# Block products for the first group's values and keys, and its queries by batch, in the opening of an attention and mixture-of-experts kernel

## The chip, the cores and the metric

The kernel runs on one core of a Trainium2 chip. The core has five engines with a queue of instructions each: TensorE (PE, matrix products), VectorE (DVE), ScalarE (ACT), GpSimd (POOL) and SyncE (SP, which issues DMA transfers). Within a queue the order is the program's. The metric is the device time of one execution in microseconds (us); the median of three runs before the change is 695.65 us.

## What is computed

Sixteen batches of 128 tokens with 256 features go through a cross attention with 16 heads of 64, and then through a top-1 mixture of eight experts with a shared expert. Keys and values come from two normalised sources, the context and the tokens ("latents"), 128 rows each; queries come from the tokens alone.

```python
def attention(x, latents, shift, scale, ln1_w, ln1_b, ln2_w, ln2_b, Wq, Wkv, Wo):
    x = layer_norm(x, ln1_w, ln1_b)                       # the context, 16 x 128 x 256
    lat = layer_norm(latents, ln2_w, ln2_b)
    lat = lat * (1.0 + scale[:, None, :]) + shift[:, None, :]
    q = einsum('bld,ed->ble', lat, Wq)
    kv = einsum('bld,ed->ble', concatenate((x, lat), axis=-2), Wkv)
    k, v = split(kv, 2, axis=-1)
    q, k, v = to_heads(q), to_heads(k), to_heads(v)       # 16 heads of 64
    logits = einsum('bhqd,bhkd->bhqk', q * attn_scale, k * attn_scale)
    out = einsum('bhqk,bhkd->bhqd', softmax(logits), v)
    return einsum('ble,de->bld', out.transpose(0, 2, 1, 3).reshape(b, n2, INNER), Wo)

x = x + attention(ctx_1024, layernorm(x), cond_1024, cond_1024, ...)
x = x + mixture_of_experts(layernorm(x), ...)
```

All data are float32.

## The kernel before

The attention goes by groups of two batches (g = 0 to 7), and each group by four steps: step u is batch u % 2 of the group and half (u // 2) % 2 of the heads. A step issues the logits of its eight heads (`logits`, L907, tile S), takes row maxima on DVE (`maxima`, L919), exponentials with sums on ACT (`exponents`, L926), divides on POOL (`normalise`, L939), transposes blocks on DVE (`turn`, L948) and sends them through memory and back with DMAs on SP's queue (`turn`, `fetch`), and ends with the product of the step before it with its values (`weigh`, L972, tile O). Between these, PE makes what later steps need: queries, keys and values.

Inputs of a group are normalised, transposed on PE and scaled into `kvT`, [128 features, chunk c, batch i, context or tokens, 128 rows]. For the first group `first_inputs(i)` does this for one batch at a time (transposes L695, tile fkvt); for the second group `inputs(1)` gives eight pieces on DVE and `transpose(c)` (tile kvt, L623); later groups are transposed through memory.

There are two ways to make keys and values. `k_plain(b, h, m)` and `v_plain(b, h, t)` multiply directly, one batch at a time: per half of the heads and group 16 instructions of 256 columns for the keys, 8 of 512 columns for the values. `Seven` makes one half for both batches of a group from seven products of blocks instead of eight (n = 1 to 7, two instructions of 256 columns each, banks X, Y and Z). It needs sums and differences of blocks of the weights (`weight_sums`, `weight_difference`, on POOL) and of the tokens (`token_sums`, POOL), and puts the products together with copies on ACT (`hold`) and sums on DVE (`join`, `join_held`). Before the change the first group uses `Seven` for its second values only (step 2); its first values and all its keys are plain.

PSUM banks come from pools: `ps_m` (tag mm) has three, `ps_s` (tag S) two, `ps_o` (tag O) one. A bank is written again only after the readers of what it held.

The order on every engine is written out by hand, `tc.manual_schedule`, so the program's order is the queue's. The opening runs: `first_inputs(0)`; four pieces of keys of batch 0 (L1322 to L1324); `first_inputs(1)`; one piece of values; the eight pieces of `inputs(1)` on DVE; the queries of both batches, four units (`q_unit`, L734); then step 0 and step 1 by `plain_step`, with the rest of the keys and values in them; step 2 and on by `seven_step`. In `first_inputs(0)` the inverse root starts from ACT's square root (L671); in `first_inputs(1)` it is found on DVE alone (`newton`). The weights are loaded on SP's queue: two quarters of the keys' weights (wk), the second batch's tokens, the other two quarters, the values' weights (wv, 1 MB), the queries' (wq, 1 MB, in the tile named early).

Of the kernel before, what the change touches and what calls it, by code (L numbers as in the profile page):

```python
# [9 lines left out]
F32 = mybir.dt.float32  # L10
# [7 lines left out]
P = 128  # L18
# [9 lines left out]
def resampler_attn__then__top1_moe_kernel(  # L28
# [476 lines left out]
    with ExitStack() as at:  # L505
# [41 lines left out]
        load_keys(0)  # L547
        load_keys(1)
        nc.sync.dma_start(out=xres[0][:, 1, :], in_=x[1])
        load_keys(2)  # L550
        load_keys(3)
        nc.sync.dma_start(
            out=wv, in_=wkv_t[:, INNER : 2 * INNER].rearrange("(c p) e -> p c e", p=P)
        )
        nc.sync.dma_start(out=wq, in_=wq_t.rearrange("(c p) e -> p c e", p=P))

        def later_loads():
            nc.sync.dma_start(out=wr[:, :, 0:E], in_=router.rearrange("(c p) e -> p c e", p=P))
# [20 lines left out]
        def inputs(g):  # L579
# [73 lines left out]
        def first_inputs(i):  # L653
# [11 lines left out]
            nc.vector.tensor_scalar(  # L665
                v[:, 1:2], mv[:, 1, 1:2], 1.0 + EPS, EPS * EPS, ALU.mult, ALU.add
            )
            if i == 0:

                root = small.tile([P, 2], F32, name="froot")  # L670
                nc.scalar.activation(root, v, AF.Sqrt)  # L671
                half = small.tile([P, 2], F32, name="fhalf")
                nc.vector.tensor_scalar(half, v, -0.5, None, ALU.mult)
                y = small.tile([P, 2], F32, name="fy")
                nc.vector.reciprocal(y, root)
                a = small.tile([P, 2], F32, name="fa")
                nc.vector.tensor_tensor(a, y, y, ALU.mult)
                nc.vector.tensor_tensor(a, a, half, ALU.mult)
                r = small.tile([P, 2], F32, name="fr")
                nc.vector.scalar_tensor_tensor(r, a, 1.5, y, ALU.add, ALU.mult)  # L680
# [66 lines left out]

        def q_unit(g, j):
            for jj in range(2):
                q_piece(g, j, jj, ps_m, "mm")  # L750
            q_keep(g, j)

        def keys_in_blocks(o, i):

# [441 lines left out]

            nc.scalar.activation(spare[0:1, 1:2], spare[0:1, 0:1], AF.Exp)

        def plain_step(u, units, side=(), behind=()):

            units, side = list(units), list(side)
# [7 lines left out]
            if u == 0 or u >= 2 * B - 2:  # L1209
                recall_exp()  # L1210
            if u > 1:
                keep_heads(u - 2)
            nm = maxima(u, 0, ps[0])
            exponents(u, 0, ps[0], nm)
            nm = maxima(u, 1, ps[1])
            if u > 1:
                exponents(u, 1, ps[1], nm)
                for n in range(2):
                    normalise(u, n)
                turn(u, 0)  # L1220
                unit(2)
                turn(u, 1)
                fetch(u)
                unit()
                weigh(u - 1)
                keep_heads(u - 1)
                unit(3)
                for f in behind:
                    f()
                finish(B - 2)  # L1230
                unit(len(units))
                return
# [12 lines left out]
            fetch(u)  # L1245
            for f in behind:
                f()
            unit()
            if u > 0:
                weigh(u - 1)  # L1250

# [79 lines left out]
        weight_sums(v_block, v_sums, 0, nc.gpsimd)  # L1331
        pieces, transpose = inputs(1)
        v_plain(0, 0, 0)
        for f in pieces:
            f()
        for j in range(4):
            q_unit(0, j)

        def second_inputs(c):
            transpose([c])  # L1340
# [4 lines left out]
        for g in range(NG):  # L1345
# [16 lines left out]
            scaled = t_on(("t_scale", 0), ("t_scale", 1))  # L1362

            if g == 0:
                turn_c = [lambda c=c: second_inputs(c) for c in range(DC)]
                ks = [lambda m=m: k_plain(1, 0, m) for m in range(2)]
                plain_step(
                    0,
                    [ks[0], turn_c[0], ks[1], turn_c[1]]
                    + [lambda: v_plain(0, 0, 1), lambda: v_plain(1, 0, 0), lambda: v_plain(1, 0, 1)],  # L1370
                )
                weight_sums(k_block, k_sums, 0, nc.gpsimd)
                token_sums(0, nc.gpsimd)
# [7 lines left out]
                seven_step(  # L1381
                    2, Seven("v", 0, 1), ask[2:], {1: kept[3]},
                    (
                        roots, (), (),
                        [lambda: token_sums(1, nc.gpsimd), lambda: weight_difference(k_block, 0, nc.gpsimd)]
                        + scaled,
                    ),
                )
                ask, kept = asking(1, 1)
                seven_step(  # L1390
                    3, Seven("k", 1, 0), ask, kept, turns,
                    on("t_fetch")
                    + [
                        lambda: weight_difference(v_block, 0, nc.gpsimd),
                        lambda: weight_sums(k_block, k_sums, 1, nc.gpsimd),
                        lambda: weight_difference(k_block, 1, nc.gpsimd),
                    ],
                )
                continue
            had_t, had_h = g + 1 < NG, g > 1  # L1400
# [22 lines left out]
            if g + 1 < NG:  # L1423
                ask, kept = asking(g + 1, 0)
                seven_step(
                    u + 2, Seven("v", g, 1), ask, kept,
                    (h_on("h_stats", "h_variances"), roots, (), ()), scaled,
                )
                ask, kept = asking(g + 1, 1)
                seven_step(  # L1430
                    u + 3, Seven("k", g + 1, 0), ask, kept, turns, t_on("t_fetch") + h_on("h_scale")
                )
            else:
                seven_step(
                    u + 2, Seven("v", g, 1), (), {}, (h_on("h_stats", "h_variances"), (), (), roots),
                    [shared_unit] * 2,
                )
                plain_step(
                    u + 3, [shared_unit] * 7, [],
                    [now["h_scale"], now["h_turn"], now["h_fetch"], spare_sums, route_consts, up_sums],  # L1440
                )
        weigh(2 * B - 1)
# [849 lines left out]
```

## Time and profile before

| | us |
|---|---|
| median of three runs (695.04 to 696.1) | 695.65 |
| the profiled execution, its own time | 695.21 |
| its span | 693.5 |
| logits of step 0, 1, 2, 3 start at | 24.5, 36.1, 45.3, 57.6 |
| wv landed | 12.0 |
| context of the second group issued on SP's queue | 12.9 |
| last product on PE ends | 687.3 |

The times in the table's last four rows are counted from the span's start. In a timeline row the first number is the start, the second the duration from the first to the last instruction of the group, then engine, line, operation, output and inputs, the shape, the number of records, and in brackets how long the engine was idle before it and what it waited for. A matmul instruction of float32 data leaves two records, a transpose one. In the first 45 us PE, DVE, ACT and POOL are busy for 43.3, 27.4, 21.9 and 19.9 us.

### The profile page before, as it was taken

How to read it: one execution, taken by the hardware profiler on the slowest of the kernel's cores; microseconds unless marked ns; L12 is line 12 of the kernel's file. 1: busy time of each engine (PE TensorE's matmuls, PEld its weight loads, DVE VectorE, ACT ScalarE, POOL GpSimd, SP SyncE). 2: the span in 40 equal slices, each digit the busy share in tenths (PEclk: the TensorE clock that was granted, in tenths of full speed). 3: DMA queues.
4: the chain of work that ended last, by engine and by line, in shares of the span. 5: the costliest groups of instructions: out<-in, count | busy, mean ns of one | idle time of the engine just before them, and what ended most of it. 6: DMA issues, size and time to landing. Idle time of an engine off the chain costs nothing.

```text
span 693.5 us, 12756 instructions
## 1 busy us (share of the span) xinstructions
PE 684.8 (99%) x4390; PEld 585.9 (84%) x4390; DVE 462.4 (67%) x1033; ACT 361.3 (52%) x1084; POOL 357.9 (52%) x549
## 2 busy tenths in 40 slices
PE   9999999999999999999999999999999999999996
PEld 6778888888888888888888887887888899988995
DVE  6667677777678688678758657647736467766520
ACT  3556466466555655655556556514436455545540
POOL 4249446546545446436435534512566477867751
PEclk9999999999999999999999999999999999999999
DMA  8255846765866685695694485543592257667513
GB/s 268 71 201 187 236 166 197 225 208 183 213 218 196 189 250 178 212 226 172 215 229 166 158 299 169 179 106 47 172 335 63 28 113 188 161 150 202 125 21 79
DMA packets 141834, 121.34 MB, mean 175 GB/s; under 512 B 61377, under 2 KB 127426, under 8 KB 141762
## 3 DMA queue, kind: packets, MB, share of 16 engines
q1 hardware_dynamic: 135602, 111.46, 52.7%
q0 software_dynamic: 5584, 8.20, 6.8%
q8 instruction: 37, 0.61, 0.4%
q10 hardware_dynamic: 576, 0.79, 0.4%
q14 instruction: 35, 0.29, 0.1%
HBM read 71.66 MB, written 48.92 MB: 174 GB/s over the span
## 4 chain that ended last, share of the span: by engine, by line
PE 91%; DVE 3%; ACT 2%; DMA 2%; issue 1%; POOL 0%; POOLq 0%; DVEq 0%; SPq 0%; ACTq 0%
PE O L972 8%; PE S L907 8%; PE pw L991 8%; PE pq L734 8%; PE rD L1858 6%; PE rX L2024 5%; PE skX L853 5%; PE svX L853 5%; PE rYZ L2024 4%; PE skZ L853 3%; PE skY L853 3%; PE svZ L853 3%; PE svY L853 3%; PE pX L307 3%; PE p L193 2%; PE pX L220 2%
## 5 line engine op out<-in xcount | busy, mean ns | idle before, releaser
L939 POOL TENSOR_SCALAR pe<-pe,rs 128x256 f32<-128x256 f32 x256 | 130.3, 527 | 212.8 <-DVE rs L936 212.8
L926 ACT ACTIVATE pe<-S,nmx 128x256 f32<-128x256 f32 x256 | 119.3, 485 | 56.5 <-DVE nmx L919 54.7
L919 DVE TENSOR_REDUCE nmx<-S 128x4 f32<-128x1024 f32 x64 | 75.3, 1218 | 26.4 <-PE S L907 26.4
L948 DVE STREAM_TRANSPOSE px<-pe 128x512 f32<-128x512 f32 x128 | 82.5, 683 | 0.7 <-POOL pe L939 0.5
L991 PE MATMUL pw<-wo,oT 128*128 128x256 f32 x256 | 66.2, 385 | 0.0
L734 PE MATMUL pq<-kvT,early 128*128 128x256 f32 x256 | 65.8, 385 | 0.0
L972 PEld LDWEIGHTS O<-pT,v 128*64 128x64 f32 x1024 | 55.2, 137 | 10.6 <-issue 6.0
L907 PE MATMUL S<-kT,qT 64*128 64x256 f32 x512 | 63.9, 389 | 0.0
L972 PE MATMUL O<-pT,v 128*64 128x128 f32 x1024 | 63.0, 276 | 0.0
L983 ACT COPY oT<-O 128x512 f32<-128x512 f32 x32 | 18.8, 587 | 84.3 <-PE O L972 84.3
L1858 PE MATMUL rD<-w,mid_w 128*128 128x256 f32 (+1 forms) x252 | 62.0, 380 | 0.0
L734 PEld LDWEIGHTS pq<-kvT,early 128*128 128x128 f32 x256 | 47.5, 190 | 11.0 <-issue 5.1
L991 PEld LDWEIGHTS pw<-wo,oT 128*128 128x128 f32 x256 | 47.5, 190 | 10.5 <-issue 4.6
L907 PEld LDWEIGHTS S<-kT,qT 64*128 64x128 f32 x512 | 46.8, 186 | 10.5 <-issue 6.2
L926 ACT ACTIVATION_READ_ACCUMULATOR pe<-S,nmx 128x1 f32 x256 | 54.8, 214 | 0.0
L936 DVE RECIPROCAL rs<-sums 128x4 f32<-128x4 f32 x64 | 11.3, 177 | 55.2 <-ACT pe L926 54.9
L2040 POOL TENSOR_TENSOR mid_w<-mid_w,hT 128x128 f32<-128x128 f32 (+2 forms) x40 | 29.4, 734 | 17.5 <-ACT mid_w L2039 17.3
L1870 POOL DMA_INDIRECT out_dram<-sg,table x18 | 29.4, 1633 | 13.5 <-DMA out_dram<-sg,table 5.6
L1858 PEld LDWEIGHTS rD<-w,mid_w 128*128 128x128 f32 (+1 forms) x252 | 32.8, 172 | 3.3 <-ACT hT L2037 0.7
L2044 DVE TENSOR_TENSOR hT<-rYZ,hT 128x256 f32<-128x256 f32 (+2 forms) x40 | 17.8, 444 | 23.8 <-ACT hT L2037 15.5
L872 ACT COPY v<-svX 128x512 f32<-128x512 f32 x45 | 26.7, 594 | 11.4 <-PE svX L853 11.1
L853 PE MATMUL svX<-wv,kvT 128*128 128x256 f32 x120 | 31.1, 382 | 0.2 <-ACT v L872 0.2
(364 smaller groups left out, 1547.8 us busy)
## 6 DMA issues: line engine op xcount, KB each, us to landing
p_blocks<-px SPq DMA_DIRECT2D x64, 512.0 KB, 2.9
pT<-p_blocks SPq DMA_DIRECT2D x64, 512.0 KB, 4.3
w<-in_w_dram SPq DMA_DIRECT2D x16, 640.0 KB, 6.4
w<-in_w_dram SPq DMA_DIRECT2D x8, 704.0 KB, 6.4
t_blocks<-tx SPq DMA_DIRECT2D x12, 256.0 KB, 2.8
kvT<-t_blocks SPq DMA_DIRECT2D x12, 256.0 KB, 6.2
out_dram<-xres SPq DMA_DIRECT2D x8, 256.0 KB, 4.7
h_rows<-h SPq DMA_DIRECT2D x8, 256.0 KB, 4.2
```

What stands on the lines that cost most here:

```text
L734: nc.tensor.matmul(pqs[g, j][:, jj], lhsT=wq[:, c, ts(2 * j + jj, P)], rhs=kvTs[g][:, c, :, 1, :], start=(c == 0), stop=(c == DC - 1),)
L853: nc.tensor.matmul(o[:, a, :], lhsT=left, rhs=right, start=(first and a == 0), stop=(a == 1), skip_group_check=True,)
L907: nc.tensor.matmul(pl[:, r, j, :], lhsT=qTs[g, h][rows, k, i, :], rhs=kTs[g, h][rows, i, k, :], start=True, stop=True,)
L919: nc.vector.tensor_reduce(nmx, pl, AX.X, ALU.max, negate=True)
L926: nc.scalar.activation(pes[u][:, h, :], pl[:, r, j, :], AF.Exp, bias=nmx[:, r, j : j + 1], accum_out=sums[u][:, h : h + 1],)
L939: nc.gpsimd.tensor_scalar(w, w, rs[:, i : i + 1], 1.0, ALU.mult, ALU.mult)
L948: nc.vector.transpose(px[:, :, t].rearrange("p j h q -> p h j q"), pes[u][:, ts(n, 4), ts(t, S)].rearrange("p h (j k) -> p h j k", k=BL),)
L972: nc.tensor.matmul(o[r * HD : (r + 1) * HD, j, :], lhsT=vs[g, h][:, i, t, ts(2 * j + r, HD)], rhs=pTs[u][:, j // 2, :, t, 2 * (j % 2) + r, :],
L991: nc.tensor.matmul(pws[b], lhsT=outT[u][:, k % HC, :], rhs=wo[:, k, :], start=(k == 0), stop=(k == NP - 1))
L1858: nc.tensor.matmul(py[0][rows, :], lhsT=mid[:, f, :], rhs=wd[:, f, :], start=(k == 0), stop=(k == NF - 1),)
L1870: add = nc.gpsimd.indirect_dma_start(out=out_rows, out_offset=Offset(ap=routing["table"][0:n, t : t + 1], axis=0), in_=py[1][0:n, :], in_o ...
L2024: nc.tensor.matmul({2: Y, 3: Z, 5: Z}.get(n, X), lhsT=lhsT, rhs=rhs, start=n in (1, 2), stop=True, skip_group_check=True,)
```

## The change

The first group's first values become a `Seven` in step 0, its second keys a `Seven` in step 1. In the opening only two pieces of keys of batch 0 are made, then the queries of batch 0 for the first half of the heads (`q_first`, products with 128 columns); the rest of the queries moves into the steps. Both batches' inverse roots start from ACT's square root. The weights are loaded in the order of first use: wq and wv ahead of the last two quarters of the keys' weights. The second group's transposes and the `q_unit`s use the O bank instead of an mm bank. `plain_step` is split: `first_step` for steps 0 and 1, `last_step` for the last one.

```diff
         load_keys(0)
         load_keys(1)
         nc.sync.dma_start(out=xres[0][:, 1, :], in_=x[1])
-        load_keys(2)
-        load_keys(3)
+        nc.sync.dma_start(out=wq, in_=wq_t.rearrange("(c p) e -> p c e", p=P))
         nc.sync.dma_start(
             out=wv, in_=wkv_t[:, INNER : 2 * INNER].rearrange("(c p) e -> p c e", p=P)
         )
-        nc.sync.dma_start(out=wq, in_=wq_t.rearrange("(c p) e -> p c e", p=P))
+        load_keys(2)
+        load_keys(3)
...
-                    pt = ps_m.tile([P, 2, 2, S], F32, tag="mm", name=f"kvt_{g}_{c}")
+                    pt = ps_o.tile([P, 2, 2, S], F32, tag="O", name=f"kvt_{g}_{c}")
...
-            if i == 0:
-
-                root = small.tile([P, 2], F32, name="froot")
-                nc.scalar.activation(root, v, AF.Sqrt)
...
-            else:
-                for r in newton(small, v, 2, "j2"):
-                    pass
+            root = small.tile([P, 2], F32, tag="froot", name=f"froot_{i}")
+            nc.scalar.activation(root, v, AF.Sqrt)
...
         def q_unit(g, j):
             for jj in range(2):
-                q_piece(g, j, jj, ps_m, "mm")
+                q_piece(g, j, jj, ps_o, "O")
             q_keep(g, j)
+
+        def q_first(j, i):
+
+            if (j, i) == (0, 0):
+                q_half(0, 0)
+            pq = ps_m.tile([P, 2, S], F32, tag="mm", name=f"fq_{j}_{i}")
+            for jj in range(2):
+                for c in range(DC):
+                    nc.tensor.matmul(
+                        pq[:, jj],
+                        lhsT=wq[:, c, ts(2 * j + jj, P)],
+                        rhs=kvTs[0][:, c, i, 1, :],
+                        start=(c == 0),
+                        stop=(c == DC - 1),
+                    )
+            nc.scalar.activation(qTs[0, 0][:, 2 * j : 2 * j + 2, i, :], pq, AF.Copy, scale=QK)
...
+        def first_step(u, seven, units, pieces):
+
+            piece = iter(pieces)
+            ps = logits(u)
+            if u == 0:
+                recall_exp()
+            nm = maxima(u, 0, ps[0])
+            exponents(u, 0, ps[0], nm)
+            nm = maxima(u, 1, ps[1])
+            units[0]()
+            for f in next(piece):
+                f()
             normalise(u, 0)
             exponents(u, 1, ps[1], nm)
-            unit()
+            units[1]()
+            for f in next(piece):
+                f()
             normalise(u, 1)
-            unit()
-            for f in side:
+            units[2]()
+            for f in next(piece):
                 f()
-            while len(units) > 1:
-                unit()
+            seven.product(1, "X")
+            seven.hold(0, 0, "X")
             turn(u, 0)
+            seven.product(5, "Z")
+            seven.hold(1, 1, "Z")
+            units[3]()
+            seven.product(6, "X", False)
+            seven.hold(0, 1, "X")
+            seven.product(2, "Y")
+            seven.join(0, 0, "Y")
             turn(u, 1)
             fetch(u)
-            for f in behind:
-                f()
-            unit()
+            units[4]()
+            seven.product(7, "X", False)
+            seven.hold(1, 0, "X")
+            seven.join_held()
+            seven.product(4, "Y")
+            seven.join(1, 0, "Y", ALU.subtract)
+            units[5]()
+            seven.product(3, "Z", False)
+            seven.join(0, 1, "Z")
             if u > 0:
                 weigh(u - 1)
...
         modulation()
         first_inputs(0)
-        for h in range(2):
-            for m in range(2):
-                k_plain(0, h, m)
-        weight_sums(v_block, v_sums, 1, nc.gpsimd)
-        weight_difference(v_block, 1, nc.gpsimd)
+        for m in range(2):
+            k_plain(0, 0, m)
+        for j in range(2):
+            q_first(j, 0)
+        weight_sums(v_block, v_sums, 0, nc.gpsimd)
+        weight_difference(v_block, 0, nc.gpsimd)
         first_inputs(1)
+        token_sums(0, nc.gpsimd)
         tokens.pop(0)
         load_tokens(1)
         later_loads()
-        weight_sums(v_block, v_sums, 0, nc.gpsimd)
         pieces, transpose = inputs(1)
-        v_plain(0, 0, 0)
-        for f in pieces:
-            f()
-        for j in range(4):
-            q_unit(0, j)
+        pieces[0]()
...
             if g == 0:
-                turn_c = [lambda c=c: second_inputs(c) for c in range(DC)]
-                ks = [lambda m=m: k_plain(1, 0, m) for m in range(2)]
-                plain_step(
-                    0,
-                    [ks[0], turn_c[0], ks[1], turn_c[1]]
-                    + [lambda: v_plain(0, 0, 1), lambda: v_plain(1, 0, 0), lambda: v_plain(1, 0, 1)],
+                idle = lambda: None
+                first_step(
+                    0, Seven("v", 0, 0),
+                    [lambda: k_plain(1, 0, 0), lambda: k_plain(1, 0, 1)]
+                    + [lambda: [q_first(j, 1) for j in range(2)], idle]
+                    + [lambda c=c: second_inputs(c) for c in range(DC)],
+                    (pieces[1:3], pieces[3:6], pieces[6:8]),
                 )
+                weight_sums(k_block, k_sums, 1, nc.gpsimd)
+                weight_difference(k_block, 1, nc.gpsimd)
+                weight_sums(v_block, v_sums, 1, nc.gpsimd)
+                weight_difference(v_block, 1, nc.gpsimd)
+                first_step(
+                    1, Seven("k", 0, 1),
+                    [idle, idle, lambda: q_unit(0, 2), lambda: q_unit(0, 3), idle]
+                    + [lambda: q_unit(1, 0)],
+                    (t_on(("t_stats", 0)), t_on(("t_stats", 1), "t_variances"), ()),
+                )
                 weight_sums(k_block, k_sums, 0, nc.gpsimd)
-                token_sums(0, nc.gpsimd)
-                plain_step(
-                    1,
-                    [lambda m=m: k_plain(1, 1, m) for m in range(2)]
-                    + [lambda: q_unit(1, 0)],
-                    t_on(("t_stats", 0), ("t_stats", 1), "t_variances"),
-                )
+                weight_difference(k_block, 0, nc.gpsimd)
...
```

`second_inputs(c)` is `transpose([c])`, and after the last chunk `load_tokens(2)`, the loads of the third group's tokens and context. In step 0 PE's order is thus: logits, two pieces of keys of batch 1, four query products of batch 1, products 1, 5, 6, 2, the first chunk's transposes, 7, 4, the second chunk's transposes, 3. In step 1: logits, `q_unit(0, 2)`, products 1 and 5, `q_unit(0, 3)`, products 6, 2, 7, 4, `q_unit(1, 0)`, product 3, and the weighting of step 0.

More of the change, by code (lines that the diff above doesn't have):

```diff
@@ L667, in first_inputs @@
             )
-            if i == 0:
-                root = small.tile([P, 2], F32, name="froot")
[L671 to L680, printed above, removed]
-            else:
-                for r in newton(small, v, 2, "j2"):
-                    pass
+            root = small.tile([P, 2], F32, tag="froot", name=f"froot_{i}")
+            nc.scalar.activation(root, v, AF.Sqrt)
+            half = small.tile([P, 2], F32, tag="fhalf", name=f"fhalf_{i}")
+            nc.vector.tensor_scalar(half, v, -0.5, None, ALU.mult)
+            y = small.tile([P, 2], F32, tag="fy", name=f"fy_{i}")
+            nc.vector.reciprocal(y, root)
+            a = small.tile([P, 2], F32, tag="fa", name=f"fa_{i}")
+            nc.vector.tensor_tensor(a, y, y, ALU.mult)
+            nc.vector.tensor_tensor(a, a, half, ALU.mult)
+            r = small.tile([P, 2], F32, tag="fr", name=f"fr_{i}")
+            nc.vector.scalar_tensor_tensor(r, a, 1.5, y, ALU.add, ALU.mult)
             z = work.tile([P, 2, D], F32, tag="z", name=f"fz_{i}", bufs=1)
@@ L1197, in recall_exp, with last_step @@
             nc.scalar.activation(spare[0:1, 1:2], spare[0:1, 0:1], AF.Exp)
-        def plain_step(u, units, side=(), behind=()):
-            units, side = list(units), list(side)
+        def last_step(u, units, behind):
+            units = list(units)
             def unit(n=1):
@@ L1208, in plain_step @@
             ps = logits(u)
[L1209 to L1212, printed above, removed]
+            recall_exp()
+            keep_heads(u - 2)
             nm = maxima(u, 0, ps[0])
@@ L1215, in plain_step @@
             nm = maxima(u, 1, ps[1])
[L1216 to L1223, printed above, removed]
-                unit()
-                weigh(u - 1)
-                keep_heads(u - 1)
-                unit(3)
-                for f in behind:
-                    f()
-                finish(B - 2)
-                unit(len(units))
-                return
@@ L1233, in plain_step @@
-            unit()
+            exponents(u, 1, ps[1], nm)
+            for n in range(2):
+                normalise(u, n)
+            turn(u, 0)
+            unit(2)
+            turn(u, 1)
+            fetch(u)
+            unit()
+            weigh(u - 1)
+            keep_heads(u - 1)
+            unit(3)
+            for f in behind:
+                f()
+            finish(B - 2)
+            unit(len(units))
+        def first_step(u, seven, units, pieces):
+            piece = iter(pieces)
+            ps = logits(u)
+            if u == 0:
+                recall_exp()
+            nm = maxima(u, 0, ps[0])
[4 more added lines that the diff above has]
+                f()
@@ L1234, in plain_step @@
             normalise(u, 0)
             exponents(u, 1, ps[1], nm)
-            unit()
+            units[1]()
+            for f in next(piece):
+                f()
             normalise(u, 1)
-            unit()
-            for f in side:
-                f()
-            while len(units) > 1:
-                unit()
+            units[2]()
+            for f in next(piece):
+                f()
+            seven.product(1, "X")
+            seven.hold(0, 0, "X")
             turn(u, 0)
+            seven.product(5, "Z")
@@ L1244, in plain_step @@
+            seven.hold(1, 1, "Z")
[4 more added lines that the diff above has]
+            seven.join(0, 0, "Y")
             turn(u, 1)
             fetch(u)
-            for f in behind:
-                f()
-            unit()
+            units[4]()
[4 more added lines that the diff above has]
+            seven.join(1, 0, "Y", ALU.subtract)
@@ L1330, in resampler_attn__then__top1_moe_kernel @@
         later_loads()
-        weight_sums(v_block, v_sums, 0, nc.gpsimd)
         pieces, transpose = inputs(1)
-        v_plain(0, 0, 0)
-        for f in pieces:
-            f()
-        for j in range(4):
-            q_unit(0, j)
+        pieces[0]()
         def second_inputs(c):
@@ L1384, in resampler_attn__then__top1_moe_kernel @@
                         roots, (), (),
-                        [lambda: token_sums(1, nc.gpsimd), lambda: weight_difference(k_block, 0, nc.gpsimd)]
-                        + scaled,
+                        [lambda: token_sums(1, nc.gpsimd)] + scaled,
                     ),
@@ L1391, in resampler_attn__then__top1_moe_kernel @@
                     3, Seven("k", 1, 0), ask, kept, turns,
[L1392 to L1397, printed above, removed]
+                    on("t_fetch"),
                 )
@@ L1437, in resampler_attn__then__top1_moe_kernel @@
                 )
-                plain_step(
-                    u + 3, [shared_unit] * 7, [],
+                last_step(
+                    u + 3, [shared_unit] * 7,
                     [now["h_scale"], now["h_turn"], now["h_fetch"], spare_sums, route_consts, up_sums],
```

## The prediction

> **What bounds the kernel now.** First the page: busy shares, and the chain that ended last.
>
> ```profile
> PE 684.8 (99%) x4390; PEld 585.9 (84%) x4390; DVE 462.4 (67%) x1033; ACT 361.3 (52%) x1084; POOL 357.9 (52%) x549
> ...
> PE 91%; DVE 3%; ACT 2%; DMA 2%; issue 1%; POOL 0%; POOLq 0%; DVEq 0%; SPq 0%; ACTq 0%
> ```
>
> TensorE (PE) is idle for 8.7 of 693.5 us, 6.2 of them after its last product (678.92 + 8.37 = 687.29). So what the first group gains or loses on PE until its third set of logits moves the end one for one. Next, PE's timeline there; the sets of logits (S, L907) are the milestones, and a bracket shows a wait.
>
> ```profile
> 7.86 7.17 PE L767 MATMUL pk<-kvT,wk 128*128 128x256 f32 x32 [0.19 <-ACT kvT L704]
> 14.87 0.60 PE L695 MATMUL fkvt<-ident,fz 128*128 128x128 f32 x4
> 15.71 1.98 PE L782 MATMUL pv<-wv,kvT 128*128 128x512 f32 x4 [0.24 <-ACT kT L774]
> 17.53 7.07 PE L734 MATMUL pq<-kvT,early 128*128 128x256 f32 x32
> 24.53 2.00 PE L907 MATMUL S<-kT,qT 64*128 64x256 f32 x16
> ...
> 30.89 5.32 PE L782 MATMUL pv<-wv,kvT 128*128 128x512 f32 x12
> 36.14 2.00 PE L907 MATMUL S<-kT,qT 64*128 64x256 f32 x16
> ...
> 45.34 2.00 PE L907 MATMUL S<-kT,qT 64*128 64x256 f32 x16
> ```
>
> The reader is to see how little PE waits: 7.2 us of keys (pk) give VectorE (DVE) time for the second batch's normalisation, and 7.1 us of queries (pq) cover the next. Third, the timelines of the helpers, for how long their chains are.
>
> ```profile
> 5.06 0.20 ACT L671 ACTIVATE froot<-fv 128x2 f32<-128x2 f32 x1 [1.81 <-DVE fv L665]
> ...
> 5.30 0.17 DVE L675 RECIPROCAL fy<-froot 128x2 f32<-128x2 f32 x1
> ...
> 6.09 0.35 DVE L140 TENSOR_SCALAR fz<-early,fmv,fr 128x128 f32<-128x128 f32 x1
> ...
> 12.78 0.88 DVE L140 TENSOR_SCALAR fz<-xres,fmv,j2y 128x128 f32<-128x128 f32 x1
> ...
> 25.71 2.36 DVE L919 TENSOR_REDUCE nmx<-S 128x4 f32<-128x1024 f32 x2 [3.73 <-PE S L907]
> ...
> 12.05 0.73 POOL L795 TENSOR_TENSOR sums_kv<-wv 128x256 f32<-128x256 f32 x1 [6.44 <-DMA wv<-in_wkv_t_dram]
> ```
>
> **The work that goes.** A matmul instruction leaves two records. The chain has 16 instructions of 256 columns in 6.91 us (0.432 us each) and 6 of 512 in 5.15 us (0.858).
> - Values, half 0: 8 x 0.858 = 6.86 us become 14 x 0.432 = 6.05: -0.81.
> - Keys, half 1: 16 x 0.432 = 6.91 become 14: -0.86.
> - Queries j = 0, 1: 8 x 0.432 = 3.46 become 16 of 128 columns. Such instructions start at 617.23, 617.45 and 617.67 us, so 0.22 each: 3.53, +0.07.
>
> Net -1.60 us. Against it stand waits, which I find by walking PE's new order with these durations and asking for each instruction what it needs.
>
> **Wait 1: the second batch's inputs.** Keys now stop after two pieces: 7.86 + 8 x 0.432 = 11.31 us. Then eight query instructions for each of j = 0, 1: to 13.07. They need wq. Before, wv landed at 12.0 us (4.3 + 7.7) with 2.6 MB issued up to it; wq now ends at 2.1 MB, at the 0.38 MB/us of those windows 1.3 us sooner: 10.7, before 11.31, so the new load order costs nothing; covered by 0.6 us of keys, and later than that one for one.
> What PE does next are the transposes of batch 1. Before, DVE found 1/sqrt by itself (Newton, nine steps to 11.4 us). Now ScalarE (ACT) takes the root, and in ACT's queue it stands behind the evacuations of both query pieces. The second can start only at 13.07 + 0.25; half the 0.60 us of L744 and the root is at 13.65. From root to first normalised piece the rows give 6.09 - 5.06 = 1.03, so 14.7; the first transpose can start at 15.05. PE is idle from 13.07: 2.0 us. The last of four pieces (0.26 apart) is done at 15.8; logits also need ACT's kvT of the first half (0.45): 16.2 us. Before there was no wait here, as four key pieces ran to 14.8 us.
> GpSimd (POOL) may stretch this. Its four weight sums begin when wv lands: 3.2 MB now instead of 2.6, so 12.7 to 13.2 us, and last 4 x 0.8 us, to about 16.2, across the four fz. The 0.88 us row above is such an overlap, against 0.35 alone. Bounds: none of the four stretched (logits at 16.2) or all, 4 x 0.53 (18.3). The sums end midway, so two: logits at 17.1. PE's loss against an unbroken 13.07 + 0.44: 2.7 to 4.8, taken 3.6 us.
> [...]
>
> **Wait 2: one bank for two transposes.** The change moves kvt (L623) from the three mm banks to the single O bank. So the second chunk's transposes wait until DVE has read the first chunk. From the end of product 2 (t), DVE does: join 0.6 after 0.2 latency, transpose for the softmax 1.23 (L948), three reads of kvt 0.43 + 0.65: free at t + 3.15. PE from t has the first four transposes 0.43 and two products 1.73: 2.16. Wait 1.0 us; up to 1.4 if POOL stretches the scaling ahead of it.
>
> **Wait 3: q_unit in the single O bank.** In step 1, pq 2 goes into O, then keys products 1 and 5, then pq 3 into the same O: it waits for ACT's copy of pq 2, which stands behind all eight exponentials. From the logits' start the rows give 25.71 - 24.53 = 1.18 to the maxima, 26.97 - 24.53 = 2.44 to the first exponential, 1.81 for each four, 0.6 for the copy: 6.7 us. PE comes there after 1.93 + 1.73 + 1.73 = 5.4. That is 1.3 us; DVE still joins the values (0.6) when the logits come, which delays the maxima by about 0.55: 1.9 us. Bounds 1.3 to 2.4.
>
> **What is moved and costs nothing.** The weight differences and k and v sums come earlier on POOL, which idles 11.9 us before its first normalisation in this stretch; they are needed more than 4 us later, and without that room each costs its 0.8 us. Products 1 to 7 need ACT's holds at 0.6 us each, covered by the product between. load_tokens(2) moves behind two block writes and two block fetches on SP: its bytes, by the last rows (issue of the second fetch 3.2 us after the last DVE transpose, 3 to 4 us to land), come at about 37 to 38 us, as DVE asks for them; behind that row stand the reciprocals and both softmax transposes, which have 2.4 us before PE needs a join. A later landing than that costs one for one.
>
> **The sum.** Before, from 7.86 to 45.34 us PE had 36.4 us of work and 1.07 of small gaps (0.1 at each change of shape, 0.4 at 15.71). After: 34.8 of work, 0.55 of gaps, waits 3.6 + 1.0 + 1.9 = 6.5: 41.85, so third logits at 49.7 instead of 45.34, +4.4; less 0.4 for what gaps and waits share (a wait swallows the gap at its place), +4.0. The profile before also has a 0.17 wait at 52.88, because the softmax of step 1 was late; it goes: +3.8. On the profiled span that is 693.5 + 3.8 = 697.3; that execution took 695.21, 0.44 below the median 695.65, so the forecast on the median is 695.65 + 3.8 = 699.4 us. With the lower bounds (2.7 + 1.0 + 1.3) it is 697.9, with the upper ones (4.8 + 1.4 + 2.4) 701.5.
>
> **Does the idle stretch slow PE's clock?** The stretch 671 to 693.5 us has a granted clock of 0.93 with 6.2 us of idleness at its end: if the lower clock is half, that is 0.07 x 22.5 / 0.5 = 3.2 us, so it fell some 3 us into the idleness. Wait 1 in one piece is 2.0 us, with the first fz stretched 2.5: under that.
> [...]
>
> **The rivals.**
> - *The saved products show.* The first logits come 8 us sooner, so ACT and DVE may be ahead of PE. It decides at the point where the three waits together are under 2.3 us (1.60 saved, 0.5 of gaps, 0.17): below, the kernel is faster, and without any wait it takes 695.65 - 2.3 = 693.4. For it: PE is the bound, and PE gets less to do. Against: the root behind two evacuations alone makes 2.7. 0.11.
> - *Two of the waits are covered.* If the single O bank is free in time (waits 2 and 3 gone), only wait 1 is left: 2.7 to 3.6 against 2.3, 696.1 to 697.0. For it: DVE's rows are idle 3.7 us ahead of L919. Against: the order on ACT is fixed, exponentials first. 0.09, most of it within 0.2% of before.
> - *The clock falls in wait 1.* If wq lands late or all fz are stretched, the idle piece passes 3 us and the next products run at half rate for as long as the opening ones did (12 records at 634 ns instead of 379, 1.3 to some 6 us): 2 us more, 701.5 to 703. 0.06.
> - *The first logits are not ten us sooner.* By the walk they are 24.53 - 17.1 = 7.4 sooner, at most 8.3; this is part of the forecast.
>
> **The numbers.** Forecast as walked 0.74, rivals 0.11, 0.09 and 0.06. 0.2% is 1.4 us, about what a measurement of this kernel can tell from no change. Faster 0.11, same 0.07, slower 0.82. Range 696.1 to 701.5: it takes in the covered rival and both bounds; the likeliest case alone has 697.9 to 701.5.
>
> **What would show it.** In the profile after: first logits at 16 to 18 us, with PE idle from about 13 and waiting on DVE's fz; a wait of about 1 us ahead of the second kvt transposes, on DVE; one of about 2 us ahead of the second pq, on ACT; third logits at 49 us; from there every step as before. Wrong would be third logits below 45 us, or a pq that does not wait.

## The result, and the profile after

The changed kernel takes 702.72 us (median of 6 runs, 700.33 to 703.28), the kernel before 695.53 us beside it (6 runs, 695.04 to 696.44). The ratio is 1.0095, with an interval of 1.0085 to 1.0105: slower by about 6.6 us (the two medians are 7.2 us apart). That is the direction forecast, but 702.72 us is 1.2 us above the upper end of the range.

First the page of the changed kernel, busy time by engine and the shares of the chain of waits:

```profile
PE 686.4 (98%) x4414; PEld 588.8 (84%) x4414; DVE 469.1 (67%) x1034; ACT 361.4 (52%) x1087; POOL 357.7 (51%) x549
...
PE 91%; DVE 4%; DMA 3%; ACT 2%; issue 1%; POOL 0%; POOLq 0%; DVEq 0%; SPq 0%; ACTq 0%
```

PE is still what the end hangs on. It has less to multiply, yet its busy time rose from 684.8 to 686.4 us: some instructions took longer. PE's timeline of the opening shows which (start, duration of the group, and in brackets the idle time ahead of it):

```profile
11.43 1.95 PE L755 MATMUL fq<-kvT,early 128*128 128x128 f32 x16
16.28 1.60 PE L690 MATMUL fkvt<-ident,fz 128*128 128x128 f32 x4 [2.91 <-DVE fz L140]
17.90 3.78 PE L918 MATMUL S<-kT,qT 64*128 64x256 f32 x16
21.61 4.00 PE L778 MATMUL pk<-kvT,wk 128*128 128x256 f32 x16
...
34.21 0.30 PE L625 MATMUL kvt<-ident,early 128*128 128x128 f32 x1 [1.05 <-DVE kvT L637]
...
35.63 2.00 PE L918 MATMUL S<-kT,qT 64*128 64x256 f32 x16
...
42.66 1.99 PE L729 MATMUL pq<-kvT,early 128*128 128x256 f32 x8 [1.38 <-ACT qT L739]
...
52.78 2.00 PE L918 MATMUL S<-kT,qT 64*128 64x256 f32 x16
```

The reader is to see three waits at the three places named ahead of the run, and one thing more: the first set of logits takes 3.78 us where the two later ones take 2.00, and the four transposes ahead of it 1.60 where four took 0.60 before. The third logits start at 52.78 us instead of 45.34, 7.44 later; from there to the end of the last product it is as before (694.53 against 687.29, 7.24 later). So nearly the whole loss arises in the first 53 us; the span is 8.1 us longer, and the remaining 0.86 lies after the last product (7.07 us against 6.21), where the change does nothing. What made that difference in this execution was not tried.

Why the instructions took longer stands in the same profile cut into windows. The columns are the window, how many microseconds it has, then busy time (and instructions) of PE, weight loads, DVE, ACT and POOL, then PE's granted clock as a share of full speed, the share of DMA and GB/s:

```profile
14.00:15.00 1.00, 0.00 (x0) 0.00 (x0) 0.90 (x4) 0.00 (x0) 0.92 (x2) 1.00 0.36 117
15.00:16.00 1.00, 0.00 (x0) 0.00 (x0) 0.89 (x2) 0.00 (x0) 0.92 (x2) 0.69 0.02 7
16.00:17.00 1.00, 0.58 (x2) 0.31 (x2) 1.00 (x4) 0.00 (x0) 0.73 (x2) 0.50 0.00 0
21.00:22.00 1.00, 1.00 (x5) 0.39 (x2) 0.52 (x2) 0.72 (x3) 0.46 (x1) 0.50 1.03 321
22.00:23.00 1.00, 1.00 (x5) 0.83 (x5) 1.00 (x2) 1.00 (x6) 0.00 (x0) 0.89 1.02 349
```

In the 15 to 16 window the mean is 0.69, so the clock fell to 0.50 at about 15.4 us; the 0.89 of 22 to 23 puts its return at 22.2. PE was idle from 13.37 (the bracket of 2.91 ends at 16.28). The clock thus fell two microseconds into the idleness, and stayed down for 6.8.

Last, the helpers ahead of that wait, in order of time:

```profile
13.69 0.20 ACT L669 ACTIVATE froot<-fv 128x2 f32<-128x2 f32 x1
13.72 0.72 POOL L806 TENSOR_TENSOR sums_kv<-wv 128x256 f32<-128x256 f32 x1 [8.03 <-DMA wv<-in_wkv_t_dram]
14.12 0.35 DVE L675 TENSOR_TENSOR fa<-fy 128x2 f32<-128x2 f32 x1
14.53 0.72 POOL L807 TENSOR_TENSOR sums_kv<-sums_kv,wv 128x256 f32<-128x256 f32 x1
14.69 0.57 DVE L678 SCALAR_TENSOR_TENSOR fr<-fa,fy 128x2 f32<-128x2 f32 x1
15.33 0.72 POOL L808 TENSOR_TENSOR sums_kv<-wv,sums_kv 128x256 f32<-128x256 f32 x1
15.37 0.76 DVE L140 TENSOR_SCALAR fz<-early,fmv,fr 128x128 f32<-128x128 f32 x1
16.01 0.73 POOL L812 TENSOR_TENSOR wv<-wv 128x256 f32<-128x256 f32 x1
16.05 0.76 DVE L140 TENSOR_SCALAR fz<-xres,fmv,fr 128x128 f32<-128x128 f32 x1
16.74 0.33 DVE L140 TENSOR_SCALAR fz<-early,fmv,fr 128x128 f32<-128x128 f32 x1
```

The root starts at 13.69 behind the second query piece, as walked. But beside POOL's sums it is not only two of the four fz that are stretched (0.76 against 0.33): two small operations ahead of them are as well. Each of the four stretched operations ends with one of POOL's sums, by the rows at 14.47 (POOL 14.44), 15.26 (15.25), 16.13 (16.05) and 16.81 us (16.74). The two fz lose 0.86 us together, less than the 2 x 0.53 = 1.06 us that the prediction took.

### The profile page after: what moved, and what is told of

It reads as the page before. It is cut to its first block, busy times and chain, and to the rows that moved or that the text cites. A ratio compares the mean times of both kernels' runs of the same rounds, so it can differ in the third digit from the quotient of the medians.

```text
span 701.6 us, 12808 instructions
## 1 busy us (share of the span) xinstructions
PE 686.4 (98%) x4414; PEld 588.8 (84%) x4414; DVE 469.1 (67%) x1034; ACT 361.4 (52%) x1087; POOL 357.7 (51%) x549
## 4 chain that ended last, share of the span: by engine, by line
PE 91%; DVE 4%; DMA 3%; ACT 2%; issue 1%; POOL 0%; POOLq 0%; DVEq 0%; SPq 0%; ACTq 0%
PE S L918 9%; PE O L983 9%; PE pw L1002 8%; PE pq L729 8%; PE rD L1888 6%; PE svX L864 5%; PE skX L864 5%; PE rX L2054 5%; PE rYZ L2054 4%; PE skY L864 4%; PE svY L864 4%; PE skZ L864 4%; PE svZ L864 4%; PE pX L307 3%; PE p L193 2%; PE pX L220 2%
## 5 line engine op out<-in xcount | busy, mean ns | idle before, releaser
L918 PE MATMUL S<-kT,qT 64*128 64x256 f32 x512 | 65.7, 397 | 0.0
L729 PE MATMUL pq<-kvT,early 128*128 128x256 f32 x240 | 62.8, 386 | 1.4 <-ACT qT L739 1.4
L729 PEld LDWEIGHTS pq<-kvT,early 128*128 128x128 f32 x240 | 44.3, 190 | 12.1 <-issue 5.0
L883 ACT COPY v<-svX 128x512 f32<-128x512 f32 x48 | 28.4, 591 | 14.5 <-PE svX L864 14.1
L864 PE MATMUL svX<-wv,kvT 128*128 128x256 f32 x128 | 33.1, 381 | 0.0
```

What stands on the lines that cost most here:

```text
L729: nc.tensor.matmul(pqs[g, j][:, jj], lhsT=wq[:, c, ts(2 * j + jj, P)], rhs=kvTs[g][:, c, :, 1, :], start=(c == 0), stop=(c == DC - 1),)
L864: nc.tensor.matmul(o[:, a, :], lhsT=left, rhs=right, start=(first and a == 0), stop=(a == 1), skip_group_check=True,)
L918: nc.tensor.matmul(pl[:, r, j, :], lhsT=qTs[g, h][rows, k, i, :], rhs=kTs[g, h][rows, i, k, :], start=True, stop=True,)
```

## The experiments

Every kernel was timed against runs of the kernel before on the same chip; there it took 696.1 to 696.3 us. A ratio of 0.001 is 0.7 us. Line numbers are those of each kernel and differ by a few lines.

**The changed kernel again.**

> The changed kernel itself once more, on the same chip and beside the same runs of the kernel before as the three others, so that the experiments can be read against it: 702 to 703 us where before is 695.5, half clock from 15 to 22 us. Nothing is tested but the spread between chips and runs.

702.29 us, ratio 1.0091 (1.0076 to 1.0106). The clock fell later here and for half as long, by the windows of this profile:

```profile
16.00:17.00 1.00, 0.66 (x3) 0.47 (x4) 1.00 (x5) 0.15 (x1) 0.09 (x1) 0.88 0.00 0
17.00:18.00 1.00, 1.00 (x4) 0.69 (x5) 0.94 (x3) 0.77 (x2) 0.00 (x0) 0.50 0.15 30
19.00:20.00 1.00, 1.00 (x8) 0.83 (x6) 0.45 (x1) 0.49 (x2) 0.92 (x2) 0.50 0.41 99
20.00:21.00 1.00, 1.00 (x7) 0.56 (x6) 0.97 (x2) 0.19 (x1) 0.92 (x2) 0.92 0.83 251
```

The clock was down from 16.8 to about 20.2 us, 3.4 us, after an idle piece of 2.87 us. So the same kernel pays for the clock differently from one execution to the next.

**Wait 1 taken away: the second batch's root on DVE again.**

```diff
-            root = small.tile([P, 2], F32, tag="froot", name=f"froot_{i}")
...
+            if i == 0:
+                root = small.tile([P, 2], F32, tag="froot", name=f"froot_{i}")
...
+            else:
+                for r in newton(small, v, 2, "j2"):
+                    pass
```

> The changed kernel with the second batch's inverse root found on DVE again (Newton), all else as changed. If wait 1 (the root behind the query evacuations on ACT) is the main loss and the lower clock its consequence: the transposes start at 13.1 us without a wait, the first logits at about 14.2 instead of 17.9, the granted clock stays at 1.00, the third logits at about 46.5 instead of 52.8, time about 696.6 us. If the clock falls for another reason (the new kernel's lighter opening, the 128-column products), the clock still falls and the time stays above 698.5. If the loss lies in the banks, the time stays above 700.

698.53 us, ratio 1.0033 (1.0021 to 1.0045). Its PE timeline:

```profile
14.34 2.00 PE L922 MATMUL S<-kT,qT 64*128 64x256 f32 x16 [0.39 <-ACT kvT L703]
...
29.07 0.30 PE L625 MATMUL kvt<-ident,early 128*128 128x128 f32 x1 [1.05 <-DVE kvT L637]
...
37.47 1.99 PE L733 MATMUL pq<-kvT,early 128*128 128x256 f32 x8 [1.33 <-ACT qT L743]
```

The first logits come at 14.34 and run at the full clock (2.00 us, and 1.00 in every window from 12 to 26 us), the other two waits stand (1.05 and 1.33 us). 0.0062 of the ratio, 4.3 us, belonged to wait 1 with the clock. The rest of the loss was larger than expected: third logits at 47.59, not 46.5. Of the 39.65 us from the first key product (7.94) to there 34.8 are work by the forecast's count and 2.98 waits in brackets (a fourth one, 0.21 us, stands ahead of the first values product); 1.87 us are small gaps, where the forecast had 0.55.

**The same by another way: statistics and root of the second batch ahead of the keys, still on ACT.**

```diff
+        first_stats(1)
         for m in range(2):
             k_plain(0, 0, m)
```

> The changed kernel with the statistics and the square root of the second batch issued ahead of the keys, so that the root is ahead of the evacuations in ACT's queue; the root stays on ACT. If it is the place in ACT's queue that costs: as with Newton, first logits at about 14.2, third at 46.5, time about 696.6. If ACT's root itself is slow for the second batch: first logits stay at 17 or later, time above 701.

698.44 us, ratio 1.0034 (1.0022 to 1.0046), first logits at 14.43. So it was the root's place in ACT's queue, not the use of ACT: either way out of that place gives the same time.

**Wait 1 kept, its idleness filled** with six constant products of 256 columns on PE. They compute nothing that is used.

```diff
+        warm_ps = ps_o.tile([P, TB], F32, tag="O", name="warm_ps")
+        for _ in range(6):
+            nc.tensor.matmul(warm_ps, lhsT=idle[:, 0, 0:P], rhs=idle[:, 0, :], start=True, stop=True)
         first_inputs(1)
```

> The changed kernel with six products of 256 columns on constants (2.6 us) between the query products and the transposes; they write a bank that nothing reads, and change no result. If the lower clock after wait 1 costs by itself: the clock stays at 1.00, the first logits still start at about 17.5 to 18, but take 1.93 us instead of 3.7, time about 2.4 us less, 700.3. If the clock is not what the opening loses: the time is the same as the changed kernel's, 702.7, or more by what the products delay.

700.79 us, ratio 1.0065 (1.0051 to 1.0079): doing more work on PE made the kernel faster by 0.0030 of the ratio against the first result, 2.1 us, with 1.2 us either way by the two intervals. Its PE timeline:

```profile
17.15 2.00 PE L918 MATMUL S<-kT,qT 64*128 64x256 f32 x16
...
49.96 2.00 PE L918 MATMUL S<-kT,qT 64*128 64x256 f32 x16
```

The logits still wait for the same inputs and start at 17.15, but they take 2.00 us, and the granted clock is 1.00 in every window from 9 to 27 us. Against this profile the changed kernel's third logits are 2.82 us late: that is the clock in an execution with 6.8 us of it, against 1.89 (51.85) in the one with 3.4, but for wait 3, which is 1.32 us here and 1.38 and 1.65 in those two.

**How much of wait 1 is POOL.** The sums of the values' weights behind the token sums:

```diff
-        weight_sums(v_block, v_sums, 0, nc.gpsimd)
-        weight_difference(v_block, 0, nc.gpsimd)
         first_inputs(1)
         token_sums(0, nc.gpsimd)
+        weight_sums(v_block, v_sums, 0, nc.gpsimd)
+        weight_difference(v_block, 0, nc.gpsimd)
```

> The sums and differences of the values' blocks on GpSimd are issued behind the token sums instead of ahead of the second batch's inputs; nothing else differs from the changed kernel. Theory (the root on ScalarE is the larger part of wait 1, GpSimd's work beside VectorE's fa, fr and fz the smaller one): fa and fr fall from 0.35 and 0.57 us to about 0.2 each, the two fz of 0.76 us to 0.55, so the fourth fz ends some 0.8 us sooner and S(0) starts at 16.3 to 17.2; PE's clock falls at about the same time as before (15.4 us), since it fell two microseconds into the idleness; total 0.5 to 1.5 us under the changed kernel, unless products with summed values then wait for their sums. Rival (the GpSimd work is what makes wait 1): S(0) at 15.5 or sooner and the clock stays up, total 3 us under the changed kernel.

701.27 us, ratio 1.007 (1.0057 to 1.0083). The two small operations fell to 0.16 us each, all four fz to 0.34, and the wait from 2.91 to 1.90 us, by the groups of DVE's instructions (busy us, mean ns of one, and idle time before) and PE's timeline:

```profile
L140 DVE TENSOR_SCALAR fz<-early,fmv,fr 128x128 f32<-128x128 f32 x2 | 0.7, 343 | 0.1
L140 DVE TENSOR_SCALAR fz<-xres,fmv,fr 128x128 f32<-128x128 f32 x2 | 0.7, 340 | 0.0
...
L678 DVE SCALAR_TENSOR_TENSOR fr<-fa,fy 128x2 f32<-128x2 f32 x1 | 0.2, 161 | 0.0
...
15.35 1.00 PE L690 MATMUL fkvt<-ident,fz 128*128 128x128 f32 x4 [1.90 <-DVE fz L140]
16.39 3.20 PE L918 MATMUL S<-kT,qT 64*128 64x256 f32 x16
```

So POOL was one microsecond of wait 1, and the root's place the larger part. The logits are slow again, and the windows say when the clock fell:

```profile
16.00:17.00 1.00, 0.96 (x8) 0.71 (x9) 0.97 (x4) 0.93 (x3) 0.08 (x1) 1.00 0.22 35
17.00:18.00 1.00, 1.00 (x8) 0.84 (x6) 0.73 (x4) 1.00 (x1) 1.00 (x2) 0.51 0.83 228
20.00:21.00 1.00, 1.00 (x5) 0.81 (x5) 1.00 (x2) 1.00 (x6) 0.92 (x2) 0.78 1.01 357
```

It fell at 17.0 us, 1.7 us after PE had resumed, and came back at 20.4. In two of the five executions (700.61 us each) the mean granted clock was 0.999 instead of 0.995. As 3.4 us at half rate alone lower the mean over 700 us by 0.0024, it can't have been down for as long there. Between the resumption and the fall stand four transposes (1.00 us) and the first 0.6 us of the logits; whether they have a part in it, no run separates. In the first profile the fall came 2.0 us into the idleness, ahead of any transpose.

**Idleness of 1.5 us:** three constant products instead of six.

```diff
-        for _ in range(6):
+        for _ in range(3):
```

> The changed kernel with three constant products instead of the six of e4_fill, ahead of the second batch's transposes, which leaves about 1.5 us of idleness there in one piece. What is open is how much idleness brings the clock down. [...] Rival (a piece of over a microsecond suffices): half clock for at least 3 us after the gap, the logits or the keys stretched, 1.5 to 3 us over e4_fill, ratio 1.0085 to 1.011.

700.68 us, ratio 1.0076 (1.0061 to 1.0092). In the profile the clock is 1.00 in every window from 14 to 23 us:

```profile
16.32 1.01 PE L690 MATMUL fkvt<-ident,fz 128*128 128x128 f32 x4 [1.52 <-DVE fz L140]
17.36 2.00 PE L918 MATMUL S<-kT,qT 64*128 64x256 f32 x16
```

Three of the four executions took 700.4 to 700.8 us at a mean clock of 0.997 or 0.998, one took 702.62 at 0.995. So 1.5 us seems mostly to do no harm; the slow one fits a fall, but it was not profiled, and the interval doesn't exclude the rival's lower end.

**The load order undone** in the kernel with the early root: the second pair of keys ahead of wq and wv.

```diff
-        nc.sync.dma_start(out=wq, in_=wq_t.rearrange("(c p) e -> p c e", p=P))
+        load_keys(2)
+        load_keys(3)
...
-        load_keys(2)
-        load_keys(3)
+        nc.sync.dma_start(out=wq, in_=wq_t.rearrange("(c p) e -> p c e", p=P))
```

> The kernel e5_root (statistics and root of the second batch ahead of the keys) with the loads in the kernel before's order: the second pair of keys ahead of the values and the queries' weights. It tells what the load order alone is worth. Theory (the order is a condition of the early query products): the queries' weights land about 4 us later, at some 14 to 15 us, so the first query product waits 3 to 5 us, S(0) starts at 17 to 19 us against 14.43 in e5_root, and the clock falls in that gap; total 3 to 6 us over e5_root. Rival (the loads are early enough in any order): S(0) within 0.5 us of e5_root and the same total.

701.42 us, ratio 1.0078 (1.0065 to 1.0091), against 1.0034 with the new order: 0.0044, or 3.1 us. PE's timeline shows where:

```profile
15.06 3.38 PE L764 MATMUL fq<-kvT,early 128*128 128x128 f32 x16 [3.55 <-DMA early<-in_wq_t_dram]
...
19.27 2.00 PE L927 MATMUL S<-kT,qT 64*128 64x256 f32 x16 [0.39 <-ACT kvT L708]
```

The query weights land 3.55 us too late, and the queries run at half clock (3.38 us instead of 1.95; it was down from 14.5 to 17.9 us). Three of the six executions took 700.5 to 701.2 us at a mean clock of 0.998, three 701.6 to 703.5 at 0.994 to 0.996, so here too the price differs from one execution to the next. The new order is a condition of the early queries.

**Waits 2 and 3: other banks.**

```diff
-                    pt = ps_o.tile([P, 2, 2, S], F32, tag="O", name=f"kvt_{g}_{c}")
+                    if c == 0:
+                        pt = ps_s.tile([P, 2, 4 * S], F32, tag="S", name=f"kvt_{g}_{c}")
+                        pt = pt[:, 0, :].rearrange("p (i t s) -> p i t s", i=2, t=2)
+                    else:
+                        pt = ps_o.tile([P, 2, 2, S], F32, tag="O", name=f"kvt_{g}_{c}")
...
+            pool, tag = (ps_m, "mm") if (g, j) == (0, 2) else (ps_o, "O")
...
-                q_piece(g, j, jj, ps_o, "O")
+                q_piece(g, j, jj, pool, tag)
```

> The changed kernel with the first chunk's kvt transposes in a bank of the logits' pool and q_unit(0, 2) in an mm bank; wait 1 stays as it is. If waits 2 and 3 come from the single O bank: the 1.05 us wait ahead of the second transposes goes, the 1.4 us wait ahead of the second pq becomes at most 0.3, time 2.2 us less than the changed kernel, 700.5. If what comes after only takes their place (holds on ACT, joins on DVE): time within 0.5 us of 702.7.

701.26 us, ratio 1.0076 (1.0062 to 1.009). Wait 2 is gone. Wait 3 has moved, by PE's timeline, from the queries to the product behind them; below it is ACT's timeline, the last exponential and what follows it:

```profile
42.31 1.10 PE L869 MATMUL skX<-kvT,sums_kv 128*128 128x256 f32 x4 [1.75 <-ACT kT L888]
...
40.60 0.51 ACT L942 ACTIVATE pe<-S,nmx 128x256 f32<-128x256 f32 x1
...
41.05 0.64 ACT L743 ACTIVATE qT<-pq 128x512 f32<-128x512 f32 x1
41.53 0.63 ACT L888 COPY kT<-skX 128x512 f32<-128x512 f32 x1
```

This product wants bank X again, and the hold that empties X stands behind the same eight exponentials. So wait 3 was not a matter of the O bank: what ACT has to empty early in step 1 stands behind the exponentials, and another bank only passes the wait on.

**All three at once:** the root by Newton, the first chunk in a logits bank, and step 1 through the routine of the later steps, which puts the copies of queries and products between the exponentials. The `q_unit`s have mm banks again. Of the edit, step 1 is shown.

```diff
-                first_step(
-                    1, Seven("k", 0, 1),
-                    [idle, idle, lambda: q_unit(0, 2), lambda: q_unit(0, 3), idle]
-                    + [lambda: q_unit(1, 0)],
-                    (t_on(("t_stats", 0)), t_on(("t_stats", 1), "t_variances"), ()),
+                ask, kept = asking(0, 1)
+                seven_step(
+                    1, Seven("k", 0, 1), ask, kept,
+                    ((), (), (), t_on(("t_stats", 0), ("t_stats", 1), "t_variances")),
+                    [lambda: q_unit(1, 0)],
```

> All three waits taken away at once: the second batch's root is made on VectorE with the iteration that the kernel before used (as in e1_newton), the first chunk of transposed keys and values has a bank of the logits' pool, and step 1 is asked through the same routine as the steps after it, with its held products ahead of the exponentials' side work, the last query unit behind them in a bank of the matrix-product pool. Theory (the products' saving of 1.6 us is real and three waits and the clock ate it): S(0) at about 14.4 us, no wait of kvt on kvT, at most 0.3 us on qT, S(2) at 44.3 to 45.3 against 45.34 in the kernel before, so 694.5 to 695.8 us where before is 695.5, a ratio of 0.998 to 1.0005. Rival A (the waits only move, as the third one moved in e2_banks): a wait of 1 us or more comes up at another product of step 1, S(2) stays at 46.5 or later, ratio 1.002 or more. Rival B (the saving of products was never there): no waits of this kind are left and S(2) still stands at 46.5.

695.81 us, ratio 0.9995 (0.9986 to 1.0004): the whole loss is gone. PE's timeline:

```profile
14.27 2.00 PE L926 MATMUL S<-kT,qT 64*128 64x256 f32 x16 [0.39 <-ACT kvT L707]
...
22.37 1.13 PE L872 MATMUL svX<-wv,kvT 128*128 128x256 f32 x4 [0.68 <-ACT kT L793]
...
31.94 1.10 PE L737 MATMUL pq<-kvT,early 128*128 128x256 f32 x4 [0.30 <-DVE kvT L641]
...
45.23 2.00 PE L926 MATMUL S<-kT,qT 64*128 64x256 f32 x16
```

From the first key product (7.87) to the third logits are 37.36 us, 1.37 of them in the three brackets, so 35.99 without; the kernel before had 37.48 with one bracket of 0.24, 37.24 without. The difference is 1.25 us: most of the forecast's saving of 1.60 is there, and small waits eat it.

**Two more banks,** for the first two of these waits.

```diff
-                    ps_s.tile([P, 2, 4 * S], F32, tag="S", name=f"fkvt_{i}_{c}_1")[:, 0, 0:S],
+                    ps_o.tile([P, S], F32, tag="O", name=f"fkvt_{i}_{c}_1")
+                    if (i, c) == (1, 0)
+                    else ps_s.tile([P, 2, 4 * S], F32, tag="S", name=f"fkvt_{i}_{c}_1")[:, 0, 0:S],
...
+            pool, tag = (ps_o, "O") if (j, i) == (1, 1) else (ps_m, "mm")
-            pq = ps_m.tile([P, 2, S], F32, tag="mm", name=f"fq_{j}_{i}")
+            pq = pool.tile([P, 2, S], F32, tag=tag, name=f"fq_{j}_{i}")
```

> e6_best with two more banks changed: the second batch's first transpose for ScalarE goes to the O bank instead of a logits bank, so that the first set of logits finds a free bank, and the second batch's second query piece goes to the O bank instead of the third matrix-product bank, so that the first values product finds one. In e6_best these two waits are 0.39 us (logits on kvT) and 0.68 us (svX on kT). Theory (every remaining wait of PE ahead of the third logits costs one for one): both are gone, S(0) at 13.9 to 14.0, S(2) at 44.1 to 44.5 against 45.23 in e6_best and 45.34 in the kernel before; about 0.9 us under e6_best, 694.7 to 695.3 where before is 696.2, a ratio of 0.998 to 0.999. Rival (VectorE, busy without a gap from 25 to 34 us in e6_best, is the bound of the two steps): the waits come back at the second chunk of kvt or at the first pq, S(2) stays at 45.0 or later, ratio 0.9995 or above.

695.39 us, ratio 0.999 (0.9981 to 0.9999), which the kernel above can't be told from. The waits of PE in its first 60 us (what waited, for what, then us in total, times, the longest):

```profile
PE svZ L875 <- ACT kT L796: 0.9, 1, 0.9
PE pq L739 <- DVE kvT L641: 0.4, 1, 0.4
PE svY L875 <- POOL sums_kv L818: 0.3, 1, 0.3
```

The first logits come at 13.70, 0.57 sooner, but waits come back, the largest one product later, and the third logits stand at 45.52, 0.29 later than in the kernel above. In this the rival was right; the ratio is at the edge of what the theory had. That VectorE is what bounds the two steps isn't shown: it is busy without a gap from 23.7 to 34.9 us there, but the largest wait is on ACT. The interval of this kernel ends at 0.9999 and that of the kernel above at 1.0004, so if either is faster than the kernel before, it is by no more than two tenths of a per cent (0.9981).

## Why the prediction missed

The cause and the direction were right, the size was not. By ratios the forecast was 1.0054 (699.4 over 695.65) and the result 1.0095. The kernel with the idleness filled, where the clock doesn't fall, stands at 1.0065. So of the 0.0041 that the forecast lacked 0.0030, 2.1 us, is the clock; the rest, 0.0011 or 0.8 us, lies within the interval of that kernel (1.0051 to 1.0079).

The step that failed is "Does the idle stretch slow PE's clock?". It gave the clock nothing, since it took from the end of the kernel before that the clock falls some 3 us into idleness, and its own idle piece was to be 2.0 to 2.5 us. Both numbers were off, and the first one decides: the clock fell 2.0 us into the idleness in one execution, and in the kernel with 1.90 us of it in one piece it fell as well. The reading of the kernel before was fair for that one execution (690 to 691 us has a clock of 0.57, so the fall came 2.85 us after the last product), but one fall is no bound. So the sum lacked a term. In the kernel with 1.90 us of idleness, just under the forecast's piece, it is about 0.8 us in three of five executions (701.4 against the 700.6 of the two others); after 2.87 and 2.91 us it is 1.89 and 2.82 at the third logits. The rival "The clock falls in wait 1" had the price (701.5 to 703) and too small a chance; and it set its point at "wq lands late or all fz are stretched", neither of which happened: PE doesn't wait for wq, and two of four fz are stretched. The records of 634 ns in the opening, from which it took the half rate, stand in windows with a granted clock of 1.00 (0 to 10 us of the kernel before), so they show no lower clock; behind wait 1 the windows do, with 0.50. Four profiles have the clock down for 3.4 us: 16.8 to 20.2 in the changed kernel again, 16.9 to 20.3 with other banks, 17.0 to 20.4 with the sums behind the token sums, 14.5 to 17.9 with the load order undone. In the first profile it was down for 6.8 us. Why it stays down for these times, no run shows.

The other steps, in the order of the text:

- PE sets the end one for one until the third logits: right (+7.44 there, +7.24 at the last product; the 0.2 between them is the wait at 52.88 that was to go).
- Net work of -1.60 us: right as work; 1.25 of it is seen, in the kernel with all three changes, once brackets are taken out.
- The new load order costs nothing: right, PE doesn't wait for wq; undone it costs 3.1 us.
- Wait 1: first logits forecast at 17.1 us. At full clock they came at 17.15, with the clock's fall at 17.90 and 17.42. The root was right to 0.04 us (13.65, measured 13.69). Two fz were stretched, as taken, but the step from the root to the first fz, 1.03 us by the rows of the first batch, became 1.68 because POOL stretched two small operations too (0.35 and 0.57 us against 0.16). That made the idle piece 2.91 instead of 2.0 to 2.5.
- Wait 2: 1.0 forecast, 1.05 in the bracket.
- Wait 3: 1.9 forecast (1.3 to 2.4), 1.38 and 1.65 in two profiles.
- Small gaps: 0.55 forecast. This was too little: 1.87 us in the kernel with the root by Newton. Part of it is about 0.15 us beside each bracket (the second transposes start 1.22 us after the product ahead of them could end, 32.13 + 2 x 0.432, where the bracket says 1.05).

Put together for the changed kernel's profile, from the same starts as the forecast: work -1.60, wait 1 at full clock 17.15 - 13.51 = 3.64, the clock 2.82, waits 2 and 3 with what lies beside their brackets 1.22 + 1.54; these make 7.62 of the 7.44 us, and -0.18 is what gaps changed elsewhere. That the saved products don't show and no two waits are covered, as the first two rivals had it, is settled by the three brackets.

## What to carry to other kernels

Work moved earlier takes its helpers along: ask for each moved product what in another engine's queue it now stands behind, for this decided every one of the three waits. When a wait leaves PE idle for two microseconds in one piece, count the slower clock after it as a likely term of its own (0.8 to 2.8 us here, after 1.90 to 2.91 us of idleness), and compare with filling the gap or with a longer chain on another engine that starts in time. Ask of a freed bank whether the engine that empties banks is the one that is late: in step 1 it was, and the wait only moved.

## What the hardware showed that was not expected

- The clock fell after 1.90 us of idleness (the kernel with the sums behind the token sums), and not during it but 1.7 us after PE had resumed. Its fall came 2.0 and 3.3 us after the idleness began in the two profiles of the changed kernel, 3.5 with other banks and 3.0 with the load order undone. It stayed down for 6.8 us in the changed kernel's first profile and for 3.4 in the four others.
- The same kernel differs with the clock from one execution to the next: 700.33 us at a mean granted clock of 0.997 and 703.28 at 0.993 among the six of the changed kernel.
- Products that compute nothing made a kernel faster by some 2 us (ratio 1.0065 against 1.0095).
- DVE operations of 128 x 2 elements beside POOL's sums took 0.35 and 0.57 us instead of 0.16. With POOL's sums moved away both took 0.16.
